# Where a state-space scan keeps its running state: SBUF or PSUM, and which engine joins two chunks

## The chip, the cores and the metric

The kernel runs on one core of one Trainium2 chip. The metric is device time in microseconds (us) for one execution, median of several. Five engines work side by side, each with its own queue that it works through strictly in order: TensorE (PE, with its weight loads as PEld), VectorE (DVE), ScalarE (ACT), GpSimd (POOL) and SyncE (SP, which here only issues transfers). They meet at semaphores. SBUF is the main on-chip memory; PSUM is the smaller one that matmuls write into; DVE and ACT also read and write it in this kernel.

## The reference

Two layers over 4096 tokens of width 256. In each, a graph layer and then a mixture of experts. The change lies in the graph layer of layer 0, in the part called Mamba, a selective state-space scan over all 4096 tokens, with 512 inner channels and 16 states for each channel:

```python
xz = h @ w_in                       # h: adjacency @ x @ gcn_w, relu, layer norm
xc, z = xz[:, :D_INNER], xz[:, D_INNER:]
u = silu(conv(xc))
dbc = u @ w_xp
dt = softplus(dbc[:, :DT_RANK] @ w_dt + b_dt)
B, C = dbc[:, DT_RANK:DT_RANK + D_STATE], dbc[:, DT_RANK + D_STATE:]
dA = exp(dt[:, :, None] * A[None])
dBu = dt[:, :, None] * B[:, None, :] * u[:, :, None]
def step(hst, inp):
    dAt, dBut, Ct = inp
    hst = dAt * hst + dBut          # the scan, token by token
    return hst, hst @ Ct
_, ys = lax.scan(step, zeros, (dA, dBu, C))
y = (ys + u * D_skip) * silu(z)
return y @ w_out
```

## The kernel before

The 4096 tokens are cut into 8 chunks of `CW` = 512. A chunk takes `STEPS` = 32 steps, 256 in all, numbered `n` through the loop at L1636; `c` is the chunk and `i` the step in it. A step works on one tile of 128 partitions, 32 channels by 4 groups of states, and on two states per partition that lie one behind the other: 1024 elements, two halves of 512. The class `Step` (L1398) holds what one step does:

- `inputs` (L1412): GpSimd multiplies dt*u by B into the tile `db` (SBUF, three buffers).
- `decays` (L1422): ScalarE writes the decays exp(dt*A) into `da`, which lies in PSUM; there are two, for even and odd steps. It makes one instruction per half. The second half leaves its first column alone: the seam between the two states, set to zero once, before the loop, on VectorE (L1568), so that one scan can run over both halves. In every chunk but the first, and for half of the steps, it first makes `e0`, the decay of the first token.
- `join` (L1435): in every chunk but the first, ScalarE adds the state carried from the chunk before, times `e0`, to the first element of the second half of `db`. (The first half gets its state through the scan's start value.)
- `scan` (L1444): VectorE runs the recurrence over the 1024 elements and writes it over `db`.
- `keep` (L1451): in every chunk but the last, ScalarE copies the last column of both halves into `state`.
- `product` (L1457): VectorE multiplies the scanned `db` by C into `hc` (SBUF, six buffers).
- `pair` (L1461): GpSimd issues a transfer that adds the second half of `hc` to the first.
- `total` (L1467): TensorE sums `hc` over states into `psy`; it follows `LAG` = 6 steps behind. `gate` (L1483) is VectorE's multiplication by silu(z).

The order in which PE, DVE, ACT and POOL get their instructions is written out by hand: it is the order of the calls (SP's is left to a scheduler). In the pass of step n the calls are: scan(n), keep(n), join(n+1), decays(n+2), VectorE's early work of the front, product(n-1), inputs(n+2), pair(n-1), gate, total, the front, tails and norms, and a share of the adjacency matmuls (`propagation`, L858).

The front (class `Front`, L900) makes dt, u, B, C and z of the next chunk while this chunk is scanned. `PLAN` (L906) says in which step each piece is issued; entries from 32 on belong to the chunk's own scan (38 is step 6). Much of it is ScalarE's: `normal` L991, `turned` L1008, `in` L1032, `silu` L1049, `abs` L1083, `exp` L1096, `plus` L1099, `log` L1109. VectorE's part of it is `stats` (L982) and the four steps of `soft` (L1112). In the last two chunks `Tail` (L1167) and `Norm` (L1235) add more ScalarE work, to finish the layer.

Of the kernel before, what the change touches and what calls it, by code (L numbers as in the profile page):

```python
# [19 lines left out]
P = 128  # L20
CW = 512
# [25 lines left out]
def kernel(ctx: ExitStack, tc: tile.TileContext, out: bass.AP, **a):  # L47
    nc = tc.nc
# [734 lines left out]
    with ExitStack() as s1:  # L783
        wp = s1.enter_context(tc.tile_pool(name="w_gnn0", bufs=1))
# [57 lines left out]
        STEPS = MB * G4 * (NS // 4) // 2  # L842
        BEGIN = 3
        BEGIN0 = 5
        LAG = 6
        W = R + 2 * NS


# [7 lines left out]
        da = [ps_a.tile([P, 2, CW], F32, name=f"da{k}", tag=f"d{k}") for k in range(2)]  # L856
# [43 lines left out]
        class Front:  # L900
# [17 lines left out]
            }  # L918
            EARLY = {
                5: ["stats 0", "stats 1", "root"],  # L920
# [240 lines left out]
        def keep_gated(c):  # L1161

            yd = dram.tile([P, MB, CW], F32, name=f"yd{c}")
            nc.sync.dma_start(yd, fronts[c].us)
            return yd
# [69 lines left out]
        class Norm:  # L1235
# [57 lines left out]
            def keep(self):  # L1293
                nc.scalar.copy(lgs[:, self.c * TPC:(self.c + 1) * TPC, :], self.ps_l)
# [103 lines left out]
        class Step:  # L1398
# [17 lines left out]
                    self.f.bc["b", self.p], ALU.mult,  # L1416
                )

            def carried(self):
                return e0[:, self.m % 2, self.q, :]  # L1420

            def decays(self):  # L1422
                m, q, p = self.m, self.q, self.p
                if self.c > 0 and p == 0:
                    nc.scalar.activation(
                        self.carried(), negA[:, q, m, 1::2], AF.Exp, scale=self.dtu[:, 0, 0:1]
                    )
                for j in range(2):
                    s_ = 2 * p + j
                    nc.scalar.activation(  # L1430
                        da[self.n % 2][:, j, j:], self.dtu[:, 0, j:], AF.Exp,
                        scale=negA[:, q, m, s_:s_ + 1],
                    )

            def join(self):  # L1435

                if self.c > 0:
                    first = self.db[:, 1, 0:1]
                    nc.scalar.activation(  # L1439
                        first, state[:, self.g, 2 * self.p + 1:2 * self.p + 2], AF.Identity,  # L1440
                        scale=self.carried()[:, self.p:self.p + 1], bias=first,
                    )

            def scan(self):  # L1444
                flat = self.db.rearrange("p a t -> p (a t)")
                nc.vector.tensor_tensor_scan(  # L1446
                    flat, da[self.n % 2].rearrange("p a t -> p (a t)"), flat,
                    state[:, self.g, 2 * self.p:2 * self.p + 1], ALU.mult, ALU.add,
                )

            def keep(self):  # L1451
                if self.c < NC - 1:
                    nc.scalar.copy(  # L1453
                        state[:, self.g, 2 * self.p:2 * self.p + 2], self.db[:, :, CW - 1]
                    )

            def product(self):  # L1457
                self.hc = w2p.tile([P, 2, CW], F32, name="hc", bufs=6)
                nc.vector.tensor_tensor(self.hc, self.db, self.f.bc["c", self.p], ALU.mult)  # L1459

            def pair(self):  # L1461
                if self.paired:
# [32 lines left out]
        with tc.manual_schedule(engines={  # L1495
# [26 lines left out]
            def advance(k=1, wait=False):  # L1522


                while k > 0:
                    k -= 1
                    if next(prop, None) and wait:
                        break
                return k
# [13 lines left out]
            negA = wp.tile([P, G4, MB, NS // G4], F32, name="negA")  # L1543
# [18 lines left out]
            carry = wp.tile([P, MB, KC - 1], F32, name="carry")  # L1562
            state = wp.tile([P, MB * G4, NS // G4], F32, name="state")
            e0 = wp.tile([P, 2, G4, 2], F32, name="e0")
            pick = wp.tile([P, 32], F32, name="pick")
            nc.vector.tensor_reduce(pick, ident.rearrange("p (c r) -> p c r", r=G4), AX.X, ALU.add)
            for k in range(2):
# [60 lines left out]
            first = fr  # L1628
            steps, tails, kept, gated, due, summed, owed = [], [], {}, [], [], 0, 0
            ALL = NC * STEPS  # L1630
# [5 lines left out]
            for n in range(ALL):  # L1636
                c, i = divmod(n, STEPS)
                cur = steps[n]
                if i == 6 and c > 0:
                    if c < NC - 1:  # L1640
                        kept[c - 1] = keep_gated(c - 1)
                    else:
                        tails.extend(Tail(c - 1, hh) for hh in range(2))
                if i == 8 and c == NC - 2:
                    tails.extend(
                        Tail(k, hh, kept[k], k < SLOW) for k in range(c) for hh in range(2)
                    )
# [12 lines left out]
                if fr is not None:  # L1660
                    if i == 27:
                        fr.states("b", 0)
                    elif i == 29:
                        fr.states("c", 0)
                    elif i == 30:
                        fr.states("b", 1)
                if i == 1 and c > 0:
                    fronts[c].states("c", 1)

                cur.scan()  # L1670
                cur.keep()
                if n + 1 < ALL:
                    steps[n + 1].join()
                if n + 2 < ALL:
                    steps.append(Step(n + 2))
                    steps[n + 2].decays()
                for f, k in live:
                    f.at(k, True)
                if c == NC - 1 and i in NORMS:
                    NORMS[i]()  # L1680
                if n > 0:
                    steps[n - 1].product()
                if n + 2 < ALL:
                    steps[n + 2].inputs()
                if n > 0:
                    steps[n - 1].pair()
                for st in gated:
                    st.gate()
                gated = []
                if summed <= n - LAG or (summed <= n - 3 and not steps[summed].paired):  # L1690
                    if steps[summed].total(steps[summed + 1]):
                        gated.append(steps[summed])
                    summed += 2
                for f, k in live:
                    f.at(k)
                for _ in range(TAILS.get((c, i), 1)):
                    Tail.step(tails)
                if c == NC - 1:
                    for piece in NPIECES.get(i, ()):
                        piece()  # L1700
                    if i == 24:
                        last = Last()
                        last.fetch()
                    elif i == 25:
                        last.first(0)
                    elif i == 27:
                        last.residual(0)
                    elif i == 29:
                        for m in range(H, MB - 1):
                            last.add(0, m)  # L1710
                if c == 0 and i < BEGIN0:
                    advance(NT // BEGIN0)
                    if i == BEGIN0 - 1:
                        advance(NT)
                        first.do_store(1)
                    continue
                at0 = c == 0 or (c == 1 and i < BEGIN)
                owed = advance((pieces0 if at0 else pieces)[i] + owed, True)
                if i == BEGIN - 1:
                    while owed:  # L1720
                        owed = advance(owed, True)
            steps[-1].product()
            last.first(1)
            for m in range(H, MB - 1):
                last.add(1, m)
# [20 lines left out]
    wp = ctx.enter_context(tc.tile_pool(name="w_ffn0", bufs=1, reuse_waits="tile"))  # L1746
# [437 lines left out]
    with tc.If(again > 0):  # L2184
        with ExitStack() as s3:
# [3 lines left out]
            with tc.For_i(0, NT, 1) as i:  # L2189
# [33 lines left out]
                for j4 in range(NT // 4):  # L2223
                    ps = ps_t.tile([P, 4, P], F32, name="ps_ta")
                    fT = gp.tile([P, 4, P], F32, name="fT_all", bufs=2)
                    for jj in range(4):
                        j = 4 * j4 + jj
                        nc.tensor.transpose(ps[:, jj, :], f[:, j * P:(j + 1) * P], ident)
                    nc.scalar.copy(fT, ps)
                    for jj in range(4):  # L2230
                        j = 4 * j4 + jj
# [103 lines left out]
```

## Time and profile before

| | us |
|---|---|
| median of three runs | 2331.31 (2326.05 to 2334.49) |
| the profiled execution, its own time | 2326.38 |
| its span | 2324.6 |
| first scan starts | 158.2 |
| last scan ends | 1269.7 |
| chunks 0 to 7, first scan to next chunk's first scan | 145.5, 139.0, 136.4, 136.3, 136.4, 136.4, 139.1, and about 143 to the last scan's end |

Busy shares over the span are PE 88%, PEld 63%, DVE 77%, ACT 56%, POOL 60%. They are averages over stages of different kind; the 1.1 ms of the scan have to be read by themselves. In the stretch from 442.7 to 988.1 us, four chunks, the chunks are alike to 0.1 us. There VectorE is busy for 129.1 us of 136.35, PE for 127, GpSimd for 103, ScalarE for 98; the granted TensorE clock is 0.95 of full speed.

How to read the lines: in a list of groups each line gives the source line, engine, operation, tile written and read, shape and count; then busy time and the mean of one; then the idle time of that engine just before these instructions and what ended it. A line of a timeline gives start and duration in us.

### The profile page before, as it was taken

How to read it: one execution, taken by the hardware profiler on the slowest of the kernel's cores; microseconds unless marked ns; L12 is line 12 of the kernel's file. 1: busy time of each engine (PE TensorE's matmuls, PEld its weight loads, DVE VectorE, ACT ScalarE, POOL GpSimd, SP SyncE). 2: the span in 40 equal slices, each digit the busy share in tenths (PEclk: the TensorE clock that was granted, in tenths of full speed). 3: DMA queues.
4: the chain of work that ended last, by engine and by line, in shares of the span. 5: the costliest groups of instructions: out<-in, count | busy, mean ns of one | idle time of the engine just before them, and what ended most of it. 6: DMA issues, size and time to landing. Idle time of an engine off the chain costs nothing. (4 is left out here: it accounts for less than half of the span.)

```text
span 2324.6 us, 28800 instructions
## 1 busy us (share of the span) xinstructions
PE 2051.4 (88%) x8851; PEld 1456.9 (63%) x8851; DVE 1791.9 (77%) x2942; ACT 1306.3 (56%) x2384; POOL 1397.2 (60%) x1061
## 2 busy tenths in 40 slices
PE   7989999999998999988588699996899989899994
PEld 6656565646555564644355588884588778778773
DVE  4977999999999999999989699413538999954342
ACT  4144668677676867768685232422488778523221
POOL 1036777786777778677764354542058778855652
PEclk9999999999999999999788799997899999999997
DMA  7667797979879797987963799873356556477894
GB/s 242 218 183 197 177 279 176 279 178 257 214 197 275 175 274 181 251 219 184 271 196 104 237 350 355 283 226 101 118 176 174 176 164 182 139 240 215 249 318 153
DMA packets 300039, 498.78 MB, mean 215 GB/s; under 512 B 32524, under 2 KB 171776, under 8 KB 298977
## 3 DMA queue, kind: packets, MB, share of 16 engines
q1 hardware_dynamic: 241760, 382.23, 51.9%
q0 software_dynamic: 58112, 114.59, 21.9%
q8 instruction: 73, 1.20, 0.2%
q14 instruction: 94, 0.76, 0.1%
HBM read 381.91 MB, written 65.80 MB: 193 GB/s over the span
## 5 line engine op out<-in xcount | busy, mean ns | idle before, releaser
L1414 POOL TENSOR_TENSOR db<-dtu,bb 128x1024 f32<-128x1024 f32 x256 | 600.9, 2348 | 276.9 <-DVE hc L1459 174.9
L1446 DVE TENSOR_TENSOR_SCAN db<-da,state,db 128x1024 f32<-128x1024 f32 x256 | 599.3, 2341 | 42.8 <-ACT db L1439 30.1
L878 PE MATMUL pt<-at,gn 128*128 128x256 f32 x2048 | 495.8, 398 | 44.0 <-DMA at<-in_adjT_dram 22.2
L878 PEld LDWEIGHTS pt<-at,gn 128*128 128x128 f32 x2048 | 397.8, 198 | 155.0 <-issue 49.8
L1430 ACT ACTIVATE da<-dtu,negA 128x512 f32<-128x512 f32 (+1 forms) x512 | 350.2, 684 | 15.5 <-DVE db L1446 3.6
L1459 DVE TENSOR_TENSOR hc<-db,cb 128x1024 f32<-128x1024 f32 x256 | 340.8, 1332 | 19.1 <-PE psy L1477 19.1
L2025 PE MATMUL pf<-gn,f 128*128 128x256 f32 x1280 | 289.2, 387 | 0.0
L2025 PEld LDWEIGHTS pf<-gn,f 128*128 128x128 f32 x1280 | 247.6, 195 | 36.8 <-issue 3.3
L712 PE MATMUL ps_h<-xkT,wk 128*128 128x256 f32 x864 | 215.2, 391 | 13.1 <-DVE xkT L737 10.7
L697 PE MATMUL ps_y<-wk,hk 128*128 128x256 f32 x864 | 212.7, 382 | 0.2
L702 DVE TENSOR_TENSOR yk<-ps_y,bk 128x512 f32<-128x512 f32 x73 | 50.2, 687 | 204.2 <-PE ps_y L697 167.2
L1463 POOL DMA_DIRECT2D hc<-hc x232 | 201.8, 870 | 0.0
L712 PEld LDWEIGHTS ps_h<-xkT,wk 128*128 128x128 f32 x864 | 159.5, 194 | 51.5 <-DVE xkT L737 18.4
L1887 POOL DMA_INDIRECT x<-gnd,ls_idx x128 | 152.3, 1190 | 60.1 <-DMA gnd<-gn 21.3
L697 PEld LDWEIGHTS ps_y<-wk,hk 128*128 128x128 f32 x864 | 161.7, 191 | 21.6 <-ACT hk L716 1.4
L1453 ACT COPY state<-db 128x2 f32<-128x2 f32 x224 | 42.8, 191 | 213.9 <-DVE db L1446 213.8
L1477 PE MATMUL psy<-hc,pick 128*32 128x256 f32 x1120 | 156.9, 408 | 0.0
L1027 PE MATMUL ps_xz<-hT,w_in 128*128 128x512 f32 x256 | 128.9, 651 | 22.5 <-ACT zs L1040 15.0
L1887 POOL DMA_INDIRECT ring<-gnd,ls_idx x88 | 110.2, 1252 | 28.7 <-issue 12.5
L716 ACT ACTIVATE hk<-ps_h,d0r_b 128x256 f32<-128x256 f32 x104 | 48.9, 473 | 137.6 <-PE ps_h L712 132.4
L1477 PEld LDWEIGHTS psy<-hc,pick 128*32 128x32 f32 x1120 | 56.9, 115 | 104.7 <-issue 74.6
L1044 PE MATMUL ps_xz<-xc,dK 128*128 128x512 f32 x256 | 115.2, 598 | 0.0
(424 smaller groups left out, 3224.5 us busy)
## 6 DMA issues: line engine op xcount, KB each, us to landing
at<-in_adjT_dram SPq DMA_DIRECT2D x208, 512.0 KB, 4.2
dtu<-dtd SPq DMA_DIRECT2D x124, 512.0 KB, 5.7
hc<-hc POOLq DMA_DIRECT2D x232, 256.0 KB, 6.0
wk<-in_L_ffn_W_dram SPq DMA_DIRECT2D x70, 512.0 KB, 6.2
wk<-in_L_ffn_expert_w_dram SPq DMA_DIRECT2D x114, 256.0 KB, 4.2
dtd<-sp SPq DMA_DIRECT2D x32, 512.0 KB, 5.3
ls_at<-in_adj_dram SPq DMA_DIRECT2D x32, 512.0 KB, 8.1
hc<-in_adj_dram SPq DMA_DIRECT2D x16, 512.0 KB, 4.6
```

The source lines that it names most:

```text
L697: nc.tensor.matmul(ps[:, j, :], hT[:, m, j * P:(j + 1) * P], w[:, m, :], start=(m == 0), stop=(m == kb_out - 1),)
L712: nc.tensor.matmul(ps[:, j, :], w[:, d, m * P:(m + 1) * P], xT[:, d, :], start=(d == 0), stop=(d == DB - 1),)
L878: nc.tensor.matmul(pt[:, k, :], xl[:, j, k * P:(k + 1) * P], at[:, jj, :], start=(j == 0 and k == 0), stop=(j == NT - 1 and k == DB - 1),)
L1027: nc.tensor.matmul(ps, w_in[:, k, m * P:(m + 1) * P], self.hT[:, k, :], start=(k == 0), stop=(k == DB - 1),)
L1414: nc.gpsimd.tensor_tensor(self.db, self.dtu[:, 1:2, :].to_broadcast([P, 2, CW]), self.f.bc["b", self.p], ALU.mult,)
L1430: nc.scalar.activation(da[self.n % 2][:, j, j:], self.dtu[:, 0, j:], AF.Exp, scale=negA[:, q, m, s_:s_ + 1],)
L1446: nc.vector.tensor_tensor_scan(flat, da[self.n % 2].rearrange("p a t -> p (a t)"), flat, state[:, self.g, 2 * self.p:2 * self.p + 1], ALU. ...
L1459: nc.vector.tensor_tensor(self.hc, self.db, self.f.bc["c", self.p], ALU.mult)
L1463: nc.gpsimd.dma_start(self.hc[:, 0, :], self.hc[:, 1, :], accum_op=ALU.add)
L1477: nc.tensor.matmul(f.psy[r, t], pick, st.hc[:, j, t], start=False, stop=(self.p == 1 and j == last and w == 1),)
L1887: nc.gpsimd.indirect_dma_start(out=to[:, :], out_offset=None, in_=gnd[:, :], in_offset=bass.IndirectOffsetOnAxis(ap=lists.idx[:, q, s:s + ...
L2025: nc.tensor.matmul(pf[:, t, :], f[:, jj, t * P:(t + 1) * P], gn[:, j, :], start=(j == 0 and t % 2 == 0), stop=(j == NT - 1 and t % 2 == 1),)
```

## The change

The scan no longer writes over `db` in SBUF but over the decays `da` in PSUM. `keep` and `product` read `da`. The product of a step is issued in that step, right behind its scan, no longer a step later; so is the pair transfer, and `LAG` goes from 6 to 5, `silu 2` from step 44 to 43 of the plan. As the scan now overwrites the seam, ScalarE sets it to zero again in each step (a copy of one column from a tile `zero`). The carried state moves to GpSimd: one multiplication of `e0` by two carried states in every other step, and one addition of one column in each.

```diff
-        LAG = 6
+        LAG = 5
...
-                39: ["in 6", "in 7"], 44: ["silu 2"],
+                39: ["in 6", "in 7"], 43: ["silu 2"],
...
             def decays(self):
-                m, q, p = self.m, self.q, self.p
+                m, q, p, d = self.m, self.q, self.p, da[self.n % 2]
                 if self.c > 0 and p == 0:
                     nc.scalar.activation(
-                        self.carried(), negA[:, q, m, 1::2], AF.Exp, scale=self.dtu[:, 0, 0:1]
-                    )
+                        e0[:, m % 2, q, :], negA[:, q, m, 1::2], AF.Exp,
+                        scale=self.dtu[:, 0, 0:1],
+                    )
+                if self.n > 1:
+                    nc.scalar.copy(d[:, 1, 0:1], zero)
...
             def join(self):
 
                 if self.c > 0:
+                    e = e0[:, self.m % 2, self.q, :]
+                    if self.p == 0:
+                        nc.gpsimd.tensor_tensor(e, e, state[:, self.g, 1::2], ALU.mult)
                     first = self.db[:, 1, 0:1]
-                    nc.scalar.activation(
-                        first, state[:, self.g, 2 * self.p + 1:2 * self.p + 2], AF.Identity,
-                        scale=self.carried()[:, self.p:self.p + 1], bias=first,
-                    )
+                    nc.gpsimd.tensor_tensor(first, first, e[:, self.p:self.p + 1], ALU.add)
 
             def scan(self):
-                flat = self.db.rearrange("p a t -> p (a t)")
+                flat = da[self.n % 2].rearrange("p a t -> p (a t)")
                 nc.vector.tensor_tensor_scan(
-                    flat, da[self.n % 2].rearrange("p a t -> p (a t)"), flat,
+                    flat, flat, self.db.rearrange("p a t -> p (a t)"),
                     state[:, self.g, 2 * self.p:2 * self.p + 1], ALU.mult, ALU.add,
                 )
 
             def keep(self):
                 if self.c < NC - 1:
                     nc.scalar.copy(
-                        state[:, self.g, 2 * self.p:2 * self.p + 2], self.db[:, :, CW - 1]
+                        state[:, self.g, 2 * self.p:2 * self.p + 2], da[self.n % 2][:, :, CW - 1]
                     )
 
             def product(self):
                 self.hc = w2p.tile([P, 2, CW], F32, name="hc", bufs=6)
-                nc.vector.tensor_tensor(self.hc, self.db, self.f.bc["c", self.p], ALU.mult)
+                nc.vector.tensor_tensor(
+                    self.hc, da[self.n % 2], self.f.bc["c", self.p], ALU.mult
+                )
...
+            zero = wp.tile([P, 1], F32, name="zero")
+            nc.gpsimd.memset(zero, 0.0)
...
                 cur.scan()
                 cur.keep()
-                if n + 1 < ALL:
-                    steps[n + 1].join()
+                cur.product()
                 if n + 2 < ALL:
                     steps.append(Step(n + 2))
                     steps[n + 2].decays()
+                    steps[n + 2].inputs()
+                cur.pair()
+                if n + 2 < ALL:
+                    steps[n + 2].join()
                 for f, k in live:
                     f.at(k, True)
                 if c == NC - 1 and i in NORMS:
                     NORMS[i]()
-                if n > 0:
-                    steps[n - 1].product()
-                if n + 2 < ALL:
-                    steps[n + 2].inputs()
-                if n > 0:
-                    steps[n - 1].pair()
                 for st in gated:
                     st.gate()
...
-            steps[-1].product()
             last.first(1)
```

More of the change, by code (lines that the diff above doesn't have):

```diff
@@ L1417, in inputs @@
                 )
-            def carried(self):
-                return e0[:, self.m % 2, self.q, :]
             def decays(self):
-                m, q, p = self.m, self.q, self.p
+                m, q, p, d = self.m, self.q, self.p, da[self.n % 2]
                 if self.c > 0 and p == 0:
                     nc.scalar.activation(
-                        self.carried(), negA[:, q, m, 1::2], AF.Exp, scale=self.dtu[:, 0, 0:1]
-                    )
+                        e0[:, m % 2, q, :], negA[:, q, m, 1::2], AF.Exp,
+                        scale=self.dtu[:, 0, 0:1],
+                    )
+                if self.n > 1:
+                    nc.scalar.copy(d[:, 1, 0:1], zero)
                 for j in range(2):
@@ L1430, in decays @@
                     nc.scalar.activation(
-                        da[self.n % 2][:, j, j:], self.dtu[:, 0, j:], AF.Exp,
-                        scale=negA[:, q, m, s_:s_ + 1],
+                        d[:, j, j:], self.dtu[:, 0, j:], AF.Exp, scale=negA[:, q, m, s_:s_ + 1]
                     )
```

## The prediction

> **What bounds the kernel now.** First the groups of instructions: two VectorE operations of each step, 256 times each, hold 940 us of the 1120 that the scan stage lasts.
>
> ```profile
> L1414 POOL TENSOR_TENSOR db<-dtu,bb 128x1024 f32<-128x1024 f32 x256 | 600.9, 2348 | 276.9 <-DVE hc L1459 174.9
> L1446 DVE TENSOR_TENSOR_SCAN db<-da,state,db 128x1024 f32<-128x1024 f32 x256 | 599.3, 2341 | 42.8 <-ACT db L1439 30.1
> L1430 ACT ACTIVATE da<-dtu,negA 128x512 f32<-128x512 f32 (+1 forms) x512 | 350.2, 684 | 15.5 <-DVE db L1446 3.6
> L1459 DVE TENSOR_TENSOR hc<-db,cb 128x1024 f32<-128x1024 f32 x256 | 340.8, 1332 | 19.1 <-PE psy L1477 19.1
> L1463 POOL DMA_DIRECT2D hc<-hc x232 | 201.8, 870 | 0.0
> L1453 ACT COPY state<-db 128x2 f32<-128x2 f32 x224 | 42.8, 191 | 213.9 <-DVE db L1446 213.8
> ```
>
> VectorE waits for little: 42.8 us before scans, 19.1 before products. Then the timeline of VectorE in a quiet stretch of chunk 3:
>
> ```profile
> 593.46 1.49 DVE L1459 TENSOR_TENSOR hc<-db,cb 128x1024 f32<-128x1024 f32 x1
> 594.87 2.34 DVE L1446 TENSOR_TENSOR_SCAN db<-da,state,db 128x1024 f32<-128x1024 f32 x1
> 597.13 1.42 DVE L1459 TENSOR_TENSOR hc<-db,cb 128x1024 f32<-128x1024 f32 x1
> 598.48 2.34 DVE L1446 TENSOR_TENSOR_SCAN db<-da,state,db 128x1024 f32<-128x1024 f32 x1
> ```
>
> The reader sees no gap: an instruction starts 0.08 us before the one ahead ends (597.13 against 594.87 + 2.34). It can, since the product belongs to the step before and needs nothing of the scan just run. A quiet step takes 3.61 to 3.67 us. Last, ScalarE in a full step of the same chunk:
>
> ```profile
> 662.25 0.19 ACT L1453 COPY state<-db 128x2 f32<-128x2 f32 x1 [0.86 <-DVE db L1446]
> 662.51 0.39 ACT L1439 ACTIVATE db<-state,db,e 128x1 f32<-128x1 f32 x1
> 662.80 1.39 ACT L1430 ACTIVATE da<-dtu,negA 128x512 f32<-128x512 f32 x2
> 664.13 0.67 ACT L1093 ACTIVATE sp<-ps_dt,b_dt 128x512 f32<-128x512 f32 x1
> ...
> 666.41 1.07 ACT L1097 ACTIVATE sp<-sp 128x1024 f32<-128x1024 f32 x1
> 667.35 0.20 ACT L1453 COPY state<-db 128x2 f32<-128x2 f32 x1
> ```
>
> `keep` is the first of its step and stands behind the whole front of the step before. In light steps it waits for the scan (213.8 us in all); here it came late, at 667.35, and nobody on VectorE needed it. That slack is what the change touches.
>
> **The change, part by part.** *The new wait.* In the program built from the changed kernel, each product of chunks 0 to 6 waits on ScalarE's semaphore, and the value is that of its own step's `keep`: two engines reading one PSUM tile are put in order. No scan waits on ScalarE any more, as the product before it has. So the path becomes scan(n), keep(n), product(n), scan(n+1), and `keep` is queued behind decays(n+1) and the front of step n-1. The decays in turn wait for product(n-1), which now reads what they overwrite. VectorE and ScalarE go in lockstep, and from the end of one product to the end of the next it takes 1.26 + max(V, S), with:
>
> V = 2.48 + E, VectorE's way: early work E, the scan 2.34 less 0.08 overlap, 0.03 until `keep` starts (597.24 on ScalarE, after 597.21), 0.19 for it.
>
> S = 1.75 + R + F, ScalarE's way: 0.03 and 0.19 for the seam copy (no such row; L1453 is the nearest at 0.191, I bound it by 0.09 and 0.39, the ends being half of it and the join's 0.387), 0.03, the decays 1.39, the front F, `keep` 0.19 less its overlap 0.07. R is 1.28 where ScalarE must load another function table first (18 such rows on L1430, 1283 ns).
>
> 1.26 = 0.03 to wake VectorE plus the product. Its form, one input in PSUM, does not occur at 1024 elements. L1485 has it at 128x512 in 0.685, L307 at 128x256 in 0.41; the straight line gives 1.23. Uncovered products from SBUF take 1.20, those that run beside GpSimd's `inputs` 1.38 to 1.53. Bounds: 1.20 and 1.49.
>
> *The sum of a chunk.* F and E are the rows of chunk 3. The floor is 32 x (1.26 + 2.48) = 119.7. What VectorE adds where it is later: stats 2.34 + gate 0.60 in step 5, soft 1.41, 1.26, 1.36, 1.37, 1.76 (with a gate), 1.26, 1.36, a gate 0.60: 13.3. What ScalarE adds, F + R - 0.73 each: biased 0.34 (F 1.07); in and normal 2.21 (2.94); in 0.34; turned 0.70; in 0.34; silu of z 2.47 (3.20); silu 0 3.08 (2.53 and R); in 0.52; silu 1 1.80; the table back 0.55; abs and exp 2.53 (3.26, the lines above), twice; plus 1.39 (2.12), twice; log 1.62 (2.35): 21.8. Silu of z, moved a step ahead, no longer shares its table with silu 0, which is in these figures. To this come 3.3 us in which ScalarE's front waited for TensorE in chunk 3 (2.6 before L1034, 0.7 before L1040), now exposed. Together 158.1, against
>
> ```profile
> 579.05:715.38 136.33, 126.92 (x505) 76.69 (x504) 129.07 (x87) 97.87 (x194) 103.30 (x65) 0.95 0.85 224
> ```
>
> a line of the table of stretches (length, then PE, PEld, DVE, ACT, POOL): +21.8. TensorE's 127 and GpSimd's 103 plus transfers fit under 158.
>
> *The other chunks.* Chunks 2 to 5: 4 x 21.8 = 87.2. Chunk 1 already has 2.7 of waits over chunk 2: about 20. Chunk 0 had VectorE waiting 6.2 us for TensorE before four products, which the slower pace covers: 15.6. Chunk 6 has tails too, puts of 0.85 and squares of 1.45 on ScalarE in steps 11 to 31, worth 7 where steps are already late, less 2.75 that it was longer before: 26. Chunk 7 has no `keep`, and so no new wait: the join's 9.2 us before its scans go, a product on its own scan starts 0.11 later (0.03 after instead of 0.08 before, as at stats to aggregate, 601.14 and 601.17) for 3.5, the product itself gives 1.7; but the decays trail the product and tails wait for TensorE up to 4.4: I take -4, bounds -8 and +4. Sum: 87.2 + 20 + 15.6 + 26 - 4 = 145.
>
> *What costs nothing.* The join on GpSimd: no row has so small an operation in the stage but pow (1.0 at best for four columns, 1.9 in this stage); memsets of one column take 0.1. I take 0.2 and 1.5 of them per step: 0.87 + 2.35 + 0.3 = 3.5 a step, under the 3.74 floor, and join(n+2) has a whole step until its scan. It stands behind pair(n), which waits for product(n), and ahead of inputs(n+3). Without that cover, at 1.0 each, GpSimd needs 4.7 in each step; see the rivals. `inputs` now needs only scan(n-1) to be done, no longer its product (the 174.9 us of the first line above), so GpSimd starts it sooner. The pair goes a step earlier with LAG one less, so TensorE finds it as before. SyncE's queue gets no new transfer, only a few in another order.
>
> *A rule against the change.* The built wait alone carries the sum above. The Trainium skill, PSUM — Partial Sum Buffer, section PSUM bank collisions raise a hardware error, says that VectorE and ScalarE may not touch one bank at once, two reads included, and that programs must guard by bank. By this the wait can't be spared as long as both read `da`; no run here shows a collision. With the rule the sum is +145, without it the second rival's -28.
>
> **The sum** stands against the profiled execution: 2326.4 + 145 = 2471. Its own time lies 5 us under the median, inside the spread of 8 of the three runs.
>
> **Rivals.** *GpSimd becomes the bound.* If its small operations cost what pow does, 4.7 x 32 = 151 per chunk, just under 158, but light steps can't run ahead by more than `db`'s three buffers: I price 7 in each of seven chunks, 2520. For: pow rows, and the 870 ns issue that stays. Against: pow is other work than an add, and GpSimd's rate on 1024 elements leaves little fixed cost.
>
> *The product does not wait* (faster). If `keep` ran at once whenever the scan ended, or the wait were for something long done, VectorE would gain the 30.1 of join waits and 256 x (1.332 - 1.23) = 26, and pay 256 x 0.11 = 28: -28, 2298. It decides if `keep` starts within 0.1 us of each scan's end. For it: 131 of 224 `keep` waited for the scan before. Against: the 93 others, and the queue order above.
>
> *ScalarE keeps up* (no change). The wait is there, but F is done in time: 119.7 + 15.1 (VectorE's extras with those of steps 21 and 22) = 134.8 a chunk, 1.5 less than before; with chunk 7, about 2312 to 2326. It decides from F below 0.73 in each step; fifteen steps of chunk 3 have more, tables counted in.
>
> **How the numbers follow.** The likeliest case 0.85, GpSimd 0.09, no wait 0.03, ScalarE keeps up 0.03. Predicted 2471. Its range: with the low ends of seam and product (0.10 and 0.03 a step, 224 steps, half of the first hidden) some 18 less, and 3.3 a chunk less if the slower pace hides TensorE's waits, about 2430; with the seam's high end where ScalarE is the later (0.1 a step on average, 22) and half of GpSimd's price (25) about 2520, which also takes that rival in. A product at 1.49 would add 58 more; those rows have both inputs in SBUF beside GpSimd, and I leave that end out at a chance of some 0.05, with 0.08 below. What can be told from no change is 0.3%, 7 us: slower 0.95, same 0.01, faster 0.04.
>
> **What would show it.** In the changed profile: products waiting for ScalarE's `keep` with some 150 to 200 us in total; quiet steps of 3.7 and steps of 6 and more where abs or silu stand; chunks of 158; products at 1.23 without the 1.4 to 1.5 ones; scans at 2.34 still; joins on GpSimd near 0.2; VectorE's busy share in chunk 3 near 0.8. It is wrong if the products wait for nothing, if scans wait for GpSimd, or if the scan on PSUM takes longer than 2.34: 0.1 us there are 26 in all.

## The result, and the profile after

The changed kernel takes 2445.11 us (median of 4 runs, 2441.87 to 2449.06); the kernel before, run beside it, takes 2330.2 us. The ratio is 1.0496, 95% interval 1.0475 to 1.0518: 115 us slower. The forecast was 2471 with a range of 2430 to 2520. The profiled execution took 2445.0 us, its span 2443.1, which is 118.5 more than the span before.

First the groups of instructions, in the form explained above:

```profile
L1414 POOL TENSOR_TENSOR db<-dtu,bb 128x1024 f32<-128x1024 f32 x256 | 641.2, 2505 | 16.3 <-DMA dtu<-sp 6.4
L1445 DVE TENSOR_TENSOR_SCAN da<-da,state,db 128x1024 f32<-128x1024 f32 x256 | 601.5, 2349 | 3.9 <-POOL db L1414 2.2
...
L1458 DVE TENSOR_TENSOR hc<-da,cb 128x1024 f32<-128x1024 f32 x256 | 313.4, 1224 | 222.9 <-ACT state L1452 210.4
...
L1427 ACT COPY da<-zero 128x1 f32<-128x1 f32 x254 | 41.2, 162 | 274.6 <-DVE hc L1458 274.6
```

The scan costs in PSUM what it cost in SBUF (2349 ns against 2341), and it waits for almost nothing now: 3.9 us. The product is cheaper (1224 against 1332), but it waits 210.4 us for ScalarE's `keep`. ScalarE in turn waits 274.6 us for the product before it may touch `da` again. Two engines wait for each other in turn; that is the lockstep.

The timeline of a quiet step of chunk 3, VectorE and ScalarE together (start, duration; in brackets the idle time before and what ended it):

```profile
641.15 2.35 DVE L1445 TENSOR_TENSOR_SCAN da<-da,state,db 128x1024 f32<-128x1024 f32 x1
...
643.53 0.16 ACT L1452 COPY state<-da 128x2 f32<-128x2 f32 x1 [0.66 <-DVE da L1445]
643.72 1.23 DVE L1458 TENSOR_TENSOR hc<-da,cb 128x1024 f32<-128x1024 f32 x1 [0.23 <-ACT state L1452]
644.86 2.35 DVE L1445 TENSOR_TENSOR_SCAN da<-da,state,db 128x1024 f32<-128x1024 f32 x1
644.98 0.16 ACT L1427 COPY da<-zero 128x1 f32<-128x1 f32 x1 [1.29 <-DVE hc L1458]
645.18 1.42 ACT L1430 ACTIVATE da<-dtu,negA 128x512 f32<-128x512 f32 x2
```

Even where ScalarE stands ready and idle (0.66 us before `keep`), VectorE loses 0.23 us between scan and product: the way to ScalarE, 0.16 us of copying, and back. The step takes 3.71 (644.86 less 641.15). Where the front has work, `keep` stands behind all of it:

```profile
762.24 1.42 ACT L1430 ACTIVATE da<-dtu,negA 128x512 f32<-128x512 f32 x2
...
763.59 0.67 ACT L1093 ACTIVATE sp<-ps_dt,b_dt 128x512 f32<-128x512 f32 x1
...
765.87 1.06 ACT L1097 ACTIVATE sp<-sp 128x1024 f32<-128x1024 f32 x1
766.82 0.17 ACT L1452 COPY state<-da 128x2 f32<-128x2 f32 x1
767.02 1.23 DVE L1458 TENSOR_TENSOR hc<-da,cb 128x1024 f32<-128x1024 f32 x1 [2.74 <-ACT state L1452]
```

These are the four `abs` pieces and the exponential that the prediction showed. Before the change `keep` came late there too and nobody on VectorE needed it; now VectorE stands still for 2.74 us. Last, chunk 3 in the table of stretches (PE, PEld, DVE, ACT, POOL, granted TensorE clock, DMA share, GB/s):

```profile
632.58:784.56 151.98, 135.69 (x505) 81.09 (x504) 125.36 (x87) 96.34 (x197) 113.13 (x115) 0.90 0.76 201
```

VectorE now works 125.4 us of 152.0 (0.82; before, 129.1 of 136.3). By chunks, against what was forecast, in us over the kernel before:

| chunk | 0 | 1 | 2 to 5 | 6 | 7 | sum |
|---|---|---|---|---|---|---|
| forecast | +15.6 | +20 | +87.2 | +26 | -4 | +145 |
| measured | +23.4 | +15.2 | +64.7 | +23.4 | -8.5 | +118.2 |

### The profile page after: what moved, and what is told of

It reads as the page before. It is cut to its first block, busy times and chain, and to the rows that moved or that the text cites. A ratio compares the mean times of both kernels' runs of the same rounds, so it can differ in the third digit from the quotient of the medians.

```text
span 2443.1 us, 28904 instructions
## 1 busy us (share of the span) xinstructions
PE 2099.2 (86%) x8851; PEld 1476.9 (60%) x8851; DVE 1761.9 (72%) x2942; ACT 1299.4 (53%) x2426; POOL 1462.8 (60%) x1398
## 4 chain that ended last, share of the span: by engine, by line
PE 33%; DVE 30%; ACT 16%; DMA 10%; issue 8%; POOL 2%; SPq 1%; DVEq 0%; POOLq 0%; ACTq 0%
PE pt L878 8%; DVE da L1445 7%; PE ps_h L712 7%; DVE hc L1458 5%; ACT da L1430 5%; PE ps_y L697 4%; DVE x L1902 3%; PE ps_xz L1027 2%; PE psy L1478 2%; DMA x<-gnd,ls_idx 2%; DVE cnt L2016 2%; DMA at<-in_adjT_dram 2%; PE pf L2024 1%; DMA yg<-d1a_ys 1%; ACT L1430 1%
## 5 line engine op out<-in xcount | busy, mean ns | idle before, releaser
L1414 POOL TENSOR_TENSOR db<-dtu,bb 128x1024 f32<-128x1024 f32 x256 | 641.2, 2505 | 16.3 <-DMA dtu<-sp 6.4
L1445 DVE TENSOR_TENSOR_SCAN da<-da,state,db 128x1024 f32<-128x1024 f32 x256 | 601.5, 2349 | 3.9 <-POOL db L1414 2.2
L878 PE MATMUL pt<-at,gn 128*128 128x256 f32 x2048 | 511.5, 408 | 48.6 <-ACT pts L884 19.4
L878 PEld LDWEIGHTS pt<-at,gn 128*128 128x128 f32 x2048 | 410.7, 204 | 162.4 <-issue 47.0
L1458 DVE TENSOR_TENSOR hc<-da,cb 128x1024 f32<-128x1024 f32 x256 | 313.4, 1224 | 222.9 <-ACT state L1452 210.4
L1464 POOL DMA_DIRECT2D hc<-hc x232 | 206.8, 891 | 293.2 <-DVE hc L1458 216.3
L1427 ACT COPY da<-zero 128x1 f32<-128x1 f32 x254 | 41.2, 162 | 274.6 <-DVE hc L1458 274.6
L1044 PE MATMUL ps_xz<-xc,dK 128*128 128x512 f32 x256 | 120.2, 619 | 10.8 <-ACT xc L1034 10.8
```

What stands on the lines that cost most here:

```text
L878: nc.tensor.matmul(pt[:, k, :], xl[:, j, k * P:(k + 1) * P], at[:, jj, :], start=(j == 0 and k == 0), stop=(j == NT - 1 and k == DB - 1),)
L1414: nc.gpsimd.tensor_tensor(self.db, self.dtu[:, 1:2, :].to_broadcast([P, 2, CW]), self.f.bc["b", self.p], ALU.mult,)
L1445: nc.vector.tensor_tensor_scan(flat, flat, self.db.rearrange("p a t -> p (a t)"), state[:, self.g, 2 * self.p:2 * self.p + 1], ALU.mult, A ...
L1458: nc.vector.tensor_tensor(self.hc, da[self.n % 2], self.f.bc["c", self.p], ALU.mult)
L1464: nc.gpsimd.dma_start(self.hc[:, 0, :], self.hc[:, 1, :], accum_op=ALU.add)
```

## Experiments

Two theories were to be told apart from the start. *The queue*: the product's wait for `keep` costs the time, since `keep` stands behind decays and front on ScalarE. *The rest*: PSUM as the scan's target, the GpSimd joins, or the new step order cost it (the last of these is the "chain theory" of the expectations). Later runs ask how far the queue theory holds in numbers, and what is left when the wait is gone. The runs of the last three headings of this section (join split, more work on ScalarE, what is left) were made on other chips, on which the kernel before takes 2381 and 2385 us; between chips only ratios are compared. Each diff is against the kernel named with it. In the expectations, e1 is the product-first version that comes next, and e4 the kernel before with the join alone on GpSimd.

### The product ahead of keep

```diff
                 cur.scan()
-                cur.keep()
                 cur.product()
+                cur.keep()
```

> The changed kernel with product(n) called ahead of keep(n), so that ScalarE's copy waits for the product and no product waits for ScalarE. Queue theory (the whole loss is the product's wait for a copy that stands behind ScalarE's front): product waits fall from 210 us to under 10, quiet steps from 3.72 to about 3.58, chunks 2 to 5 from 152 to 128 to 134 (TensorE's 127 to 134 us of work may bind), time 2285 to 2320, under the 2330 of before. Chain theory (the loss comes from a product that must follow its own scan, and from decays that must follow the product, in the same step): chunks stay near 150 and the time above 2420.

Measured, against the changed kernel: 2351.36 us, ratio to the kernel before 1.0102 (1.0062 to 1.0142). No product waits for ScalarE any more; of the 66.3 us of idle time that are left before products, 47.4 end with TensorE:

```profile
L1458 DVE TENSOR_TENSOR hc<-da,cb 128x1024 f32<-128x1024 f32 x256 | 313.4, 1224 | 66.3 <-PE psy L1478 47.4
```

Quiet steps take 3.58 us. Swapping two calls, with the same instructions on each engine, takes back 94 of the 115 us (92, if one goes by the ratios). So the loss is an order: which of two readers of one PSUM tile goes first. What is left did not come out as expected: chunks 2 to 5 take 139.6 to 140.2 us, more than the 128 to 134 of the expectation, and the time is above the forecast 2285 to 2320. One step is conspicuous, step 29 of chunks 1 to 6 with 8.56 us (6.34 in the kernel before, so 13 us more in all), in this timeline of GpSimd and VectorE:

```profile
715.69 2.66 POOL L1414 TENSOR_TENSOR db<-dtu,bb 128x1024 f32<-128x1024 f32 x1
715.76 3.68 DVE L1115 TENSOR_TENSOR t<-t,sp 128x1024 f32<-128x1024 f32 x1 [1.36 <-ACT state L1452]
```

A VectorE operation that takes 1.22 us elsewhere takes 3.68. Both engines began within 0.07 us; it ends 1.09 us after GpSimd's ends (719.44 and 718.35). The other large part of what is left is chunk 6, 149.9 us against 139.1 before; there and in chunk 0 fall 24.3 of the 47.4 us of waits for TensorE. The next run shows the long VectorE operation again, in every step.

### The new order, but scan, keep and product on SBUF

```diff
-                if self.n > 1:
-                    nc.scalar.copy(d[:, 1, 0:1], zero)
...
-                flat = da[self.n % 2].rearrange("p a t -> p (a t)")
+                flat = self.db.rearrange("p a t -> p (a t)")
...
-                    flat, flat, self.db.rearrange("p a t -> p (a t)"),
+                    flat, da[self.n % 2].rearrange("p a t -> p (a t)"), flat,
...
-                    self.hc, da[self.n % 2], self.f.bc["c", self.p], ALU.mult
+                    self.hc, self.db, self.f.bc["c", self.p], ALU.mult
```

The diff is against the changed kernel; `keep` reads `db` too, and the order of all calls stays.

> The changed kernel's order (product behind its own scan, LAG 5, join on GpSimd), but scan, keep and product work on db in SBUF as before, and the seam is set once. keep still stands ahead of the product in the order of calls. Queue theory: two reads of an SBUF tile do not order the engines, so no product waits for ScalarE; chunks of 128 to 140, time 2300 to 2350, products that run beside GpSimd's inputs again 1.4 to 1.5. Chain theory: as slow as the changed kernel, above 2420, since the order of the steps is the same.

Measured: 2480.97 us, ratio 1.0658 (1.0616 to 1.07), slower than the changed kernel itself. The products do not wait for ScalarE in this run: in the programs built here, two engines that read one tile are put in order where it lies in PSUM and not where it lies in SBUF. That part was as the queue theory has it. Its time, 2300 to 2350, failed: the run lies above 2420, where the chain theory had it. A step takes some 5.05 us, for a reason that neither theory had:

```profile
676.37 2.35 POOL L1414 TENSOR_TENSOR db<-dtu,bb 128x1024 f32<-128x1024 f32 x1
677.12 2.69 DVE L1456 TENSOR_TENSOR hc<-db,cb 128x1024 f32<-128x1024 f32 x1
679.73 2.34 DVE L1443 TENSOR_TENSOR_SCAN db<-da,state,db 128x1024 f32<-128x1024 f32 x1
680.10 0.89 POOL L1462 DMA_DIRECT2D hc<-hc  x1 [1.38 <-DVE hc L1456]
```

The product, with both inputs in SBUF, runs beside GpSimd's `inputs` and ends 1.09 us after it (679.81 and 678.72): it stood still until GpSimd was done. Over all steps the product takes 2.16 us on average. Then `pair` waits for the product (255.7 us in all), `inputs` stands behind `pair` and the join in GpSimd's queue, and the next product waits for `inputs`: a circle of some 5.05 us. In the changed kernel the product runs beside `inputs` just as much and takes 1.23, since one of its inputs is in PSUM. So the new step order needs the PSUM tile, and the PSUM tile brings the wait.

### The product ahead of keep, the join back on ScalarE

```diff
-                    if self.p == 0:
-                        nc.gpsimd.tensor_tensor(e, e, state[:, self.g, 1::2], ALU.mult)
                     first = self.db[:, 1, 0:1]
-                    nc.gpsimd.tensor_tensor(first, first, e[:, self.p:self.p + 1], ALU.add)
+                    nc.scalar.activation(
+                        first, state[:, self.g, 2 * self.p + 1:2 * self.p + 2], AF.Identity,
+                        scale=e[:, self.p:self.p + 1], bias=first,
+                    )
...
                 cur.keep()
+                if n + 1 < ALL:
+                    steps[n + 1].join()
...
-                if n + 2 < ALL:
-                    steps[n + 2].join()
```

This is the product-first version, with `join(n+1)` behind `keep(n)` on ScalarE again.

> e1 with the join given back to ScalarE, issued behind keep(n) as before the change. Now scan(n+1) waits for join(n+1), which stands behind keep(n), which waits for product(n). Queue theory: ScalarE's queue is on VectorE's path again, some 0.5 us in each step and the front's excess over about 1.4 us on top: chunks near 150, time 2400 to 2450. Rival (the place of the join does not matter as long as the product is free): within 15 us of e1.

Measured: 2402.76 us, ratio 1.0314 (1.0276 to 1.0352), 51 us over the product-first version, as the queue theory had it. The waits of VectorE (reason, total, times, longest) name the place:

```profile
DVE da L1446 <- ACT db L1439: 94.1, 128, 3.4
```

Scans wait for the join, which in this order starts only once `keep` may read `da`, after the product. Where no front delays the join, VectorE stands for 0.51 us before the scan, and the step takes 4.18 us instead of 3.58. In the changed kernel and here, a small operation of VectorE's path that was put on ScalarE cost the way there and back at the least (0.23 and 0.51 us of standing in quiet steps), and ScalarE's queue on top.

### The kernel before, with the join alone on GpSimd

```diff
                 if self.c > 0:
+                    e = self.carried()
+                    if self.p == 0:
+                        nc.gpsimd.tensor_tensor(e, e, state[:, self.g, 1::2], ALU.mult)
                     first = self.db[:, 1, 0:1]
-                    nc.scalar.activation(
...
+                    nc.gpsimd.tensor_tensor(first, first, e[:, self.p:self.p + 1], ALU.add)
...
-                if n + 1 < ALL:
-                    steps[n + 1].join()
...
                     steps[n - 1].pair()
+                if n + 2 < ALL:
+                    steps[n + 2].join()
```

Against the kernel before: scan in SBUF, product a step later, only the join moved.

> The kernel before with one part of the change alone: the join on GpSimd, issued behind pair(n-1). If the join on ScalarE cost what the scans waited for it (30.1 us), the time falls to 2300 to 2315. Rival: GpSimd, whose queue now has 0.3 to 0.8 us more in each step and waits in pair for the product, makes the scans wait instead: 2325 or more.

Measured: 2304.4 us, ratio 0.9898 (0.986 to 0.9936). It beats both kernels; of what the change does, this is the part that gains. Chunk 3 in the table of stretches, and two steps on GpSimd and VectorE:

```profile
572.17:705.45 133.28, 124.56 (x506) 75.48 (x505) 125.33 (x87) 87.50 (x162) 122.89 (x114) 0.97 0.90 229
```

```profile
604.19 0.89 POOL L1463 DMA_DIRECT2D hc<-hc  x1
604.79 0.60 POOL L1440 TENSOR_TENSOR e<-e,state 128x2 f32<-128x2 f32 x1
605.46 0.19 POOL L1442 TENSOR_TENSOR db<-db,e 128x1 f32<-128x1 f32 x1
605.60 2.36 POOL L1414 TENSOR_TENSOR db<-dtu,bb 128x1024 f32<-128x1024 f32 x1
605.69 2.35 DVE L1446 TENSOR_TENSOR_SCAN db<-da,state,db 128x1024 f32<-128x1024 f32 x1 [0.36 <-POOL db L1442]
607.90 0.87 POOL L1463 DMA_DIRECT2D hc<-hc  x1
```

`inputs` now begins with the scan and is over as the product begins, so the product takes 1.236 on average instead of 1.332; VectorE's work falls from 129.1 to 125.3 us a chunk. So the time came out inside the expected 2300 to 2315, but by luck, not for the reason given: the 30.1 us that scans waited for the join on ScalarE became 26.1 on GpSimd, while the shorter products give 256 times 0.096, or 25 us. The reader also sees the next bound: GpSimd has no gap, and a step with the multiplication of `e` takes it 3.82 us, against 3.55 without. Its scans wait for the join.

### The join split between ScalarE and GpSimd

```diff
+                if self.c > 0 and p == 0:
+                    e = self.carried()
+                    for k in range(2):
+                        nc.scalar.activation(
+                            e[:, k:k + 1], state[:, self.g, 2 * k + 1:2 * k + 2], AF.Identity,
+                            scale=e[:, k:k + 1],
+                        )
...
-                    if self.p == 0:
-                        nc.gpsimd.tensor_tensor(e, e, state[:, self.g, 1::2], ALU.mult)
```

Against the version just shown: the multiplication goes to ScalarE behind the decays, where no one waits for it soon; GpSimd keeps the addition.

> e4 (before, with the join on GpSimd) with the multiplication of e0 by the carried state given back to ScalarE, behind the decays, as two instructions in every other step; GpSimd keeps the one addition. In e4 steps with that multiplication take 3.82, those without it 3.55: if GpSimd's 0.5 us there makes the product run into the next inputs, these 14 or so steps of a chunk fall to 3.6, 3 to 4 us a chunk, 20 to 28 in all: 2276 to 2285. Rival (ScalarE, late in the steps of the front, holds up the join and with it GpSimd's queue): no gain, 2300 or more.

Measured: ratio 0.9876 (0.9838 to 0.9914), not to be told from 0.9898; the expected gain of 20 to 28 us did not come. The steps did go from 3.82 to 3.55, and the join's waits before scans fell from 26.1 to 1.7 us. The gain went to TensorE:

```profile
DVE hc L1464 <- PE psy L1482: 32.0, 26, 2.3
```

Products wait 32.0 us for TensorE to give back an `hc` buffer, 10.7 in the version before. At some 133 us a chunk TensorE, with 125 to 127 us of work, looks like the next bound; that was not tested, and the two versions ran on different chips.

### More work on ScalarE

```diff
+            nc.gpsimd.memset(junk, 0.0)
...
                     steps[n + 2].decays()
+                    for _ in range(2):
+                        nc.scalar.copy(junk, junk)
```

Against the changed kernel: two copies of a scratch tile of 128x256 onto itself, behind the decays of each step.

> The changed kernel with more work for ScalarE: two copies of a scratch tile, 128x256 each, behind the decays of each step, some 0.6 us of F together (the tile is used for nothing else). Law of the prediction, a step takes the later of VectorE's way and ScalarE's: quiet steps stay at 3.72, since they have 0.66 us of slack there (ScalarE's idle time ahead of its state copy); the fifteen or so late steps of a chunk get 0.5 to 0.6 more each, 7 to 9 us in a chunk; seven chunks with a state copy make 50 to 65, time 2495 to 2515. Rival (a wait costs only its round trip of 0.23, the front is hidden): under 15 more. Rival (ScalarE's time adds in each step): 0.55 x 224 = 125 more.

Measured: 2607.72 us, ratio 1.0942 (1.0904 to 1.098), 0.0446 above the changed kernel's ratio or some 104 us. The expectation was 50 to 65. The size was misjudged: the two copies take more than was reckoned, more steps are late, and chunk 7, which was left out of the sum, grew by 11 us. But the pattern by steps is the theory's. A quiet step and a late one:

```profile
681.38 2.35 DVE L1445 TENSOR_TENSOR_SCAN da<-da,state,db 128x1024 f32<-128x1024 f32 x1
...
683.04 0.82 ACT L1681 COPY junk<-junk 128x256 f32<-128x256 f32 x2
683.77 0.15 ACT L1452 COPY state<-da 128x2 f32<-128x2 f32 x1
683.96 1.22 DVE L1458 TENSOR_TENSOR hc<-da,cb 128x1024 f32<-128x1024 f32 x1 [0.23 <-ACT state L1452]
...
819.05 1.23 DVE L1458 TENSOR_TENSOR hc<-da,cb 128x1024 f32<-128x1024 f32 x1 [3.49 <-ACT state L1452]
```

Each pair of copies holds ScalarE for 0.73 us (683.77 less 683.04). In the quiet step they fill the 0.66 us in which ScalarE was idle, and the product's wait stays 0.23. In the step of the `abs` pieces the wait grows from 2.74 (at 767.02 in the changed kernel) to 3.49, by 0.75. Over the 32 steps of chunk 3, sixteen grew by 0.72 to 0.77, three by 0.37 to 0.49 (ScalarE had less slack there than the copies take), and thirteen not at all: 13.3 us in all. Had every step paid, it would be 32 x 0.73 = 23.4. This is max(V, S) of the forecast, read step by step: work on ScalarE is free up to the point where ScalarE is later than VectorE, and counts in full beyond it.

### What is left of the product-first version

Two runs took up the 47.4 us for which its products wait for TensorE. Both diffs are against the product-first version. The first gives `hc` a seventh buffer, and `db` one less to make room:

```diff
-                self.db = w2p.tile([P, 2, CW], F32, name="db", bufs=3)
+                self.db = w2p.tile([P, 2, CW], F32, name="db", bufs=2)
...
-                self.hc = w2p.tile([P, 2, CW], F32, name="hc", bufs=6)
+                self.hc = w2p.tile([P, 2, CW], F32, name="hc", bufs=7)
```

> e1 (product ahead of keep) with seven hc buffers in place of six, paid for with two db buffers in place of three. In e1 the products still waited 47.4 us for TensorE to give back an hc buffer. If that wait is what keeps e1 1% over before, the time falls by 30 to 45, to 2305 to 2325. If VectorE is late there because TensorE or ScalarE is behind anyway, the wait moves to another place and the time stays within 12 us of e1's 2351.

Measured: ratio 1.0132 (1.01 to 1.0163), no gain. The waits for TensorE before products are gone, but with two `db` buffers `inputs` can only begin when the scan ends, and it meets the operations of `soft`:

```profile
692.80 2.37 POOL L1414 TENSOR_TENSOR db<-dtu,bb 128x1024 f32<-128x1024 f32 x1 [2.03 <-DVE da L1445]
...
693.95 2.30 DVE L1117 TENSOR_TENSOR sp<-sp,t 128x1024 f32<-128x1024 f32 x1
```

Again the VectorE operation ends 1.08 us after GpSimd's (696.25 and 695.17). Since two things were changed at once, this run does not price the TensorE waits. The second run sums a step earlier:

```diff
-        LAG = 5
+        LAG = 4
...
-                39: ["in 6", "in 7"], 43: ["silu 2"],
+                39: ["in 6", "in 7"], 42: ["silu 2"],
```

> The product-first version (product ahead of keep in ScalarE's and VectorE's order) with LAG 4 instead of 5, and 'silu 2' in step 42 of the plan instead of 43 so that it stays ahead of its gate. In the product-first version 24 products waited 47.4 us in all for TensorE's sums of the steps whose hc buffer they take over. Theory: what is left of the loss there is this wait, and TensorE's sums come late by their place in its queue. Then with the sums one step earlier the waits fall under 15 us, chunks 2 to 5 take 135 to 138 us instead of 139.6 to 140.2, and the ratio to the kernel before is 0.995 to 1.004. Rival: the sums are late since TensorE is full (129 us of 139.6); then the place in the queue moves the wait to other work (ScalarE's front waits for TensorE, soft operations late), and the ratio stays at 1.008 to 1.015.

and the product-first version again, beside it on one chip:

> The product-first version again, on the chip of the LAG 4 run, so that the two are compared side by side. Expected: ratio 1.006 to 1.014 as on the first chip, products waiting for TensorE for 40 to 55 us, quiet steps of 3.58.

Measured: ratio 1.007 (1.0044 to 1.0096) with `LAG` 4, and 1.0097 (1.0065 to 1.0128) for the repetition, which confirms the 1.0102 of the first chip. The two intervals overlap: a small gain at best. The waits of VectorE with `LAG` 4:

```profile
DVE us L1486 <- ACT state L1452: 19.1, 5, 4.8
DVE hc L1458 <- PE psy L1478: 13.0, 6, 9.0
...
DVE us L1486 <- ACT zs L1051: 8.3, 3, 4.4
```

The products' waits fall from 47.3 to 13.0 us, as the first theory said, but gates (`us`) now wait 27 us behind the silu of z, which had to move ahead with them (4.5 us in the repetition); chunks 2 to 5 take 138.2 to 140.2, not 135 to 138. So TensorE's place in its queue was a part of it, and the rest moved. Step 29 costs 8.56 in both, 13 us more than before over chunks 1 to 6. That the conflict with GpSimd in that step is what keeps this version from passing the kernel before (16 us, by the ratio) is argued from these numbers and was not tried alone; it stays open.

## Why the prediction was right, point by point

**The wait** is the one forecast: products wait for `keep`, 210.4 us, a little more than the "some 150 to 200". 221 times 0.23 us, or 51, is the bare way to ScalarE and back; the other 159 are decays and front ahead of `keep`. Without the wait (product first) 94 of 115 us come back; with more work on ScalarE it grows just in the steps where ScalarE is later.

**The quiet step** was put at 3.74 and takes 3.72. The product was put at 1.23 from two narrower rows with one input in PSUM, and takes 1.224. The scan in PSUM was left at 2.34 and takes 2.349.

**What was to cost nothing** did: scans wait 2.2 us for GpSimd in all; the addition of the join takes 0.19 us alone and 0.50 where it runs beside the transfer's issue, and `inputs` starts early enough. The rival in which GpSimd becomes the bound fell. So did the two faster ones, by the 210 us and by the late steps: in chunk 3 products waited for longer than the bare 0.23 us in sixteen of 32 steps, so ScalarE was the later in these sixteen. (`keep` shows a wait for its scan 14 times, the second line below; in the two steps that remain, both came at about the same time.)

**The chunk** was mis-sized, 158.1 against 152.0. The term that failed first is the "3.3 us in which ScalarE's front waited for TensorE in chunk 3, now exposed". ScalarE's waits in that chunk after the change are these and no others:

```profile
ACT da L1427 <- DVE hc L1458: 36.0, 30, 1.3
ACT state L1452 <- DVE da L1445: 17.0, 14, 3.0
```

At the slower pace TensorE is done in time. Second, the extra work of both engines was 2.2 us too dear: the operations of `soft` were priced at their former 1.26 to 1.41 a step, and add 1.13 each, no longer meeting GpSimd (1.2 us over six of them); and of the gates, a step earlier with `LAG` 5, one more falls into a step where ScalarE is late anyway (0.6); the small rest is ScalarE's. The floor gave the last 0.6 (32 times 0.02). 3.3 + 2.2 + 0.6 = 6.1. ScalarE's own terms came out closely: 2.47 and 3.08 were forecast for the silu of z and silu 0, and from one product to the next these two steps took 2.45 and 3.09 more than the quiet 3.72. Over chunks 2 to 5 this is the difference between 87.2 and 64.7, less 2 us.

**Chunk 0** was too cheap: 15.6 against 23.4. The step that failed is "the slower pace covers" the waits for TensorE. It didn't, because ScalarE stood waiting for TensorE with `keep` queued behind:

```profile
187.43 0.58 ACT L884 COPY pts<-pt 128x512 f32<-128x512 f32 x1 [9.64 <-PE pt L878]
187.91 0.17 ACT L1452 COPY state<-da 128x2 f32<-128x2 f32 x1
188.11 1.23 DVE L1458 TENSOR_TENSOR hc<-da,cb 128x1024 f32<-128x1024 f32 x1 [9.70 <-ACT state L1452]
...
207.42 1.22 DVE L1458 TENSOR_TENSOR hc<-da,cb 128x1024 f32<-128x1024 f32 x1 [12.11 <-ACT state L1452]
```

The same mechanism, one engine further: VectorE now inherits whatever ScalarE's queue waits for.

**Chunk 7** gained 8.5, just past the bound of -8. VectorE's busy time there fell by 7.2 us (129.3 to 122.1), and 6.4 of that was not in the sum: a few small operations of `Norm` and the routing took 12.2 us before and take 5.8 now. By their operands it is the lock of the last section, and the trace agrees: before, seven of them ran beside GpSimd's `inputs` and ended 0.01 to 0.16 us after it; after the change three did. It was not tried alone. (The product's own gain in the recorded sum, 1.7, is 0.9 by its row there, 1258 ns against 1.23 us.) One of them in chunk 7, in the list of groups, of the kernel before and of the changed one:

```profile
L177 DVE TENSOR_TENSOR d_oh<-d_rev,rt_red 128x128 bf16<-128x128 f32 x1 | 1.9, 1893 | 0.0
```

```profile
L177 DVE TENSOR_TENSOR d_oh<-d_rev,rt_red 128x128 bf16<-128x128 f32 x1 | 0.3, 273 | 0.0
```

**The sum** came out 26 us under the 2471, inside the range, whose low end had allowed for the 3.3 us a chunk that TensorE's waits did not cost. There was some luck in it: for chunks 1 to 7 the forecast was too high by 34 us together, and chunk 0, too low by 7.8, hid a part of that. The 1120 us that the prediction gives for the scan stage are 1111.5 from the first scan's start to the last one's end; nothing in the sum rests on it.

## What to carry to other kernels

Before two engines are made to read one PSUM tile, look which of them the order lets in first, and what stands ahead of that one in its own queue: here a copy of 0.16 us, placed first on a loaded engine, cost 94 us, and the swap of two calls gave them back. A step that is put on a second engine is free only while that engine is the earlier one, so count it in each step and not by its mean share; in chunk 3 ScalarE was busy for 63% of the time and still late in sixteen steps of 32. And take a change apart: of this one, the join on GpSimd alone makes the kernel 1% faster (0.9898, 0.986 to 0.9936).

## What the runs showed of the hardware that was not expected

*VectorE stands still beside GpSimd, by operands.* An operation of 128x1024 with both inputs in SBUF that starts while GpSimd's multiplication from SBUF is running ends 1.07 to 1.10 us after the latter, whenever it began (98 of 98 in the chunks read of six versions, where more than 0.1 us of the multiplication was left): it took 2.30, 2.69 and 3.68 us instead of 1.22 in the three timelines above. With one input in PSUM (the product of the changed kernel) it takes 1.22 to 1.23 beside the same work. In the version with the join back on ScalarE, operations of `soft` that started 0.97 to 1.09 us ahead of the multiplication took their usual 1.21 to 1.22; one product of the SBUF version that started only 0.23 ahead was held all the same and took 3.96. The Trainium skill, SBUF — State Buffer, section Who interferes with whom, says that a VectorE instruction with two SBUF inputs contends with a GpSimd instruction that reads SBUF, and calls the ports that they share an exclusive lock; the times of this case agree with it. The kernel before shows it too, in the steps that the prediction quotes. These are GpSimd's lines there:

```profile
591.52 2.34 POOL L1414 TENSOR_TENSOR db<-dtu,bb 128x1024 f32<-128x1024 f32 x1 [0.51 <-DVE hc L1459]
595.13 2.34 POOL L1414 TENSOR_TENSOR db<-dtu,bb 128x1024 f32<-128x1024 f32 x1 [0.45 <-DVE hc L1459]
```

They end at 593.86 and 597.47; the two products of 1.49 and 1.42 us end at 594.95 and 598.55, 1.09 and 1.08 later. The prediction took the former 1.38 to 1.53 of such products as a mild slowing and did not see the lock behind it.

*The granted TensorE clock was lower where the same matrix work was spread over a longer chunk.* In chunk 3 of seven versions (join alone on GpSimd, the kernel before, product first, product first with the join on ScalarE, the changed kernel, scan and product on SBUF, more work on ScalarE) the chunk took 133.3, 136.3, 139.6, 146.5, 152.0, 162.4 and 165.3 us, and the clock was 0.97, 0.95, 0.94, 0.92, 0.90, 0.89 and 0.88. TensorE's busy share does not give this order: 88.4% went with 0.92, 89.3% with 0.90. TensorE was busy for 124.6 us of the first and 140.2 of the last. Which of the two sets the other was not tried, and the last of the seven ran on another chip.
